# Gathering expert slots in columns by seven products instead of row by row, in a fused attention and soft-MoE kernel

## The chip, the cores and the metric

One core of a Trainium2 chip runs the kernel. The time is device microseconds of one execution; runs of the kernel before lay between 424.82 and 426.81 us. Work is shared by TensorE (PE in the profile; PEld are its weight loads), VectorE (DVE), ScalarE (ACT), GpSimd (POOL) and SyncE (SP), which issues the transfers. Each engine takes its instructions in order, and a semaphore wait holds up all that is queued behind it.

## The reference, cut to what matters

Two batches of 1024 tokens of 256 numbers go through a cross attention, a grouped feed forward, a sigmoid cross attention and last a soft mixture of experts, each added onto the input. The change lies in the last:

```python
xn = rms_norm(layernorm(x), gamma_x)            # (b, 1024, 256)
se = rms_norm(slot_embeds, gamma_slot)          # 8 x 128 = 1024 slots
logits = einsum('bsd,etd->bset', xn, se)
dispatch = softmax(logits, axis=1)              # over the tokens
slots = einsum('bsd,bset->betd', xn, dispatch)  # gather: (b, 1024 slots, 256)
h = gelu(slots @ w1)                            # 256 -> 1024
processed = h @ w2                              # 1024 -> 256
combine = softmax(logits over all slots)
out = einsum('bnd,bsn->bsd', processed, combine)
```

## The kernel before

All is in float32. A batch's 1024 tokens are eight tiles of 128; `xh` holds the normalised tokens (without gamma_x), `xhT` the same transposed, `seT` the transposed slots with the gammas folded in. The last layer runs per batch b through these stages:

- `logits(b, s)`: for token tile s, two PSUM banks of 512 slots (4 matmuls of 512 columns, L256); DVE stores the negated logits to `lg` with the row's minimum and keeps the running maximum over the tokens in `rmax`; ACT writes the exponentials for the combine weights to `ec` (L279), with their row sums in `zc`.
- `largest`/`spread` (batch 0, with TensorE) or `largest_by_moves`/`spread_by_moves` (batch 1, with transfers) turn `rmax` into `mb`, the maximum of each slot in all partitions. `less` adds `mb` to a tile of `lg` (L395; on POOL, three tiles of batch 1 on DVE), and `dispatch` takes the exponential in place on ACT (L398).
- `gather(b, c)`: slots 128 at a time, c = 0 to 7. Eight matmuls (L409, output `psl`) use a 128 x 128 piece of `lg` as weights and `xh` as moving operand. `xh` is 258 wide: two columns of ones give the sum of the exponentials beside each slot. DVE divides by that sum. Chunks 0 to 3 are transposed by DVE and two transfers, chunks 4 to 7 by TensorE (`turn_slots`, L450, output `pst`), with gamma_x multiplied in.
- `hidden(b)`: slots @ w1 and gelu, by Strassen-Winograd's seven products of halves (28 matmuls of 512 columns, L515, `pmh_a`, `pmh_b`, `pmh_c`); `sum_slots` and `sum_weights` make the sums of halves. A product that shares terms is added onto the bank of another, in PSUM.
- `processed(b)`: h @ w2, and `combined(b)`: the combine with `ec`, seven products each (112 matmuls of 128 columns each, L616, `pp` and `pc`). The sums of halves of their operands are made by DVE (L627), in place.
- `turn(q, h)` transposes a half of four tiles of `ec` for `combined`: four DVE transpositions (L308) and 16 transfers on SP (L325).

The order on TensorE is that of the code: logits of both batches, gather(0), hidden(0), processed(0), combined(0), then the same for batch 1. Inside `tc.manual_schedule` the engines that are named keep the order in which the code issues; elsewhere a scheduler orders them, ACT excepted in this last layer. While gather(0) runs, POOL and DVE take away the maxima of batch 1 and ACT takes its exponentials, so that all of batch 1's `lg` is ready long before gather(1). On ACT, `dispatch(1, 7)` stands ahead of hidden(0)'s first copy (L545).

Of the kernel before, what the change touches and what calls it, by code (L numbers as in the profile page):

```python
# [44 lines left out]
XW = D + 2  # L45
SQ = 32
R4 = P // SQ
IN_ORDER = {mybir.EngineType.DVE, mybir.EngineType.PE}
# [4 lines left out]
def tile_kernel(  # L53
# [50 lines left out]
    gx = const.tile([P, DC], FP, name="gx")  # L104

# [110 lines left out]
    def norm_tokens(q):  # L216
# [12 lines left out]
        xh = keep[q // QB].tile([P, QT, XW], FP, tag=f"xh_{q % QB}", name=f"xh_{q}")  # L229
        nc.gpsimd.memset(xh[:, :, D:XW], 1.0)  # L230
        for t in range(QT):
            nc.vector.tensor_scalar(
                xh[:, t, 0:D], xq[q][:, t, :], mv[:, t, 0:1], f[:, t : t + 1],
                ALU.subtract, ALU.mult,
            )
        xhs[q] = xh

    def turn_tokens(q):
        xhT = pools["mw"].tile([P, DC, QN], FP, tag="xhT", name=f"xhT_{q}", bufs=3)
        tr = pools["mw"].tile([P, R4, DC, QT, SQ], FP, tag="tr", name=f"tr_m_{q}", bufs=2)  # L240
        turned(xhs[q], xhT, tr)
        xhTs[q] = xhT

    def logits(b, s):
# [5 lines left out]
        lg = keep[b].tile([P, NSLOT], FP, tag=f"lg_{s}", name=f"lg_{b}_{s}")  # L250
        lgs[b][s] = lg
        nm = stat.tile([P, 2], FP, tag="nm", name=f"nm_{b}_{s}")
        for n in range(NSLOT // 512):
# [16 lines left out]
            if s == 1:  # L270
                nc.vector.scalar_tensor_tensor(
                    rm, lgs[b][0][:, ts(n, 512)], -1.0, pl, ALU.mult, ALU.max
                )
            elif s > 1:
                nc.vector.tensor_tensor(rm, rm, pl, ALU.max)  # L275
        if t == 0:

            ecs[q] = keep[b].tile([P, 2, QT, 512], FP, tag=f"ec_{q % QB}", name=f"ec_{q}")
# [9 lines left out]
    trs = {}  # L288

    def turn(q, h, late=False, move=True):  # L290
# [4 lines left out]
        if q < QB:  # L295
            tr = pools["m12"].tile(
                [P, R4, EC // 2, QT, SQ], FP, tag="tr", name=f"tr_{q}_{h}", bufs=2
            )
        else:

            if h == 0:
                trs[q] = keep[0].tile(
                    [P, 2, R4, EC // 2, QT, SQ], FP, tag=f"ec_{q % QB}", name=f"tr_{q}"
                )
            tr = trs[q][:, h]
        half = ecs[q][:, h]
        for t in range(QT):
            ins = nc.vector.transpose(  # L308
# [3 lines left out]
            if late:  # L312
                tc.keep_in_program_order(ins)
        turned_squares[q, h] = tr
        if move:
            turn_moves(q, h)

    turned_squares = {}

    def turn_moves(q, h):  # L320
        half, tr = ecs[q][:, h], turned_squares[q, h]
# [8 lines left out]
    def largest(b):  # L330
# [9 lines left out]
        dg = diagonals[:, 0, 0 : EC * SQ].rearrange("p (c n) -> p c n", c=EC)  # L340
# [8 lines left out]
    def spread(b):  # L349

        mb = pools["md"].tile([P, NSLOT], FP, tag="mb", name=f"mb_{b}")
        to = mb.rearrange("p (c i n) -> p i c n", c=EC, i=R4)
# [12 lines left out]
        mbs[b] = mb  # L365

    moved = {}

    def largest_by_moves(b):

        w = pools["slp"].tile([P, DC, NSLOT], FP, tag="slT", name=f"max_{b}")
        sq = w[:, 0, :]
        nc.vector.transpose(sq, rmaxs[b])
# [19 lines left out]
    def less(b, s):  # L393
        engine = nc.vector if b == 1 and s in (3, 4, 5) else nc.gpsimd
        engine.tensor_tensor(lgs[b][s], lgs[b][s], mbs[b], ALU.add)  # L395
# [4 lines left out]
    slTs, prs, pts, sls, hss, m12s = {}, {}, {}, {}, {}, []  # L400

    pzs, trs_sl, gx_row, m1_sums = {}, {}, [], []

    def gather_from(b, c, tiles):
        if c not in pzs:
            pzs[c] = bank(f"psl_{b}_{c}", 0)
        pz = pzs[c]
        for s in tiles:
            nc.tensor.matmul(  # L409
                pz[:, 0:XW],  # L410
                lhsT=lgs[b][s][:, ts(c, P)],
                rhs=xhs[b * QB + s // QT][:, s % QT, :],
                start=(s == 0),
                stop=(s == ST - 1),
            )

    def gather(b, c):

        if b == 0 and c == 0:

            for tiles in (range(4), range(4, ST)):
                for i in range(3):
                    gather_from(b, i, tiles)
        elif b > 0 or c > 2:
            gather_from(b, c, range(ST))
        pz = pzs.pop(c)
        rz = stat.tile([P, 1], FP, tag="rz", name=f"rz_{b}_{c}")
        nc.vector.reciprocal(rz, pz[:, D : D + 1])
        sl = pools["m12"].tile([P, D], FP, tag="sl", name=f"sl_{b}_{c}", bufs=2)
        if c >= QT:  # L430
            nc.vector.tensor_scalar(sl, pz[:, 0:D], rz, None, ALU.mult)
            sls[c] = sl
            return

        nc.vector.scalar_tensor_tensor(sl, pz[:, 0:D], rz, gx_row[0], ALU.mult, ALU.mult)
        if c == 0:
            trs_sl[b] = pools["md"].tile(
                [P, R4, DC, QT, SQ], FP, tag="rmax", name=f"tr_sl_{b}"
            )
        square(sl, trs_sl[b], c)  # L440
        if c == QT - 1:
            from_squares(trs_sl[b], slTs[b][0], f"sl_{b}")

    def turn_slots(b, c):

        if c % 2 == 0:
            pts[c // 2] = bank(f"pst_{b}_{c // 2}", 1)
        pt = pts[c // 2]
        for dc in range(DC):
            nc.tensor.transpose(  # L450
                pt[:, ds(dc * 2 * P + (c % 2) * P, P)], sls[c][:, ts(dc, P)], ident
            )
        if c == EC - 3:
            for dc in range(DC):
                slots_out(b, c // 2, dc)

    def slots_out(b, c2, dc):
        nc.vector.tensor_scalar(
            slTs[b][1][:, dc, ts(c2 - 2, 2 * P)], pts[c2][:, ts(dc, 2 * P)],
            gx[:, dc : dc + 1], None, ALU.mult,  # L460
        )

    lefts, rights = [], {}
# [13 lines left out]
    def sum_slots(b):  # L480

        x, y = slTs[b]
        b11, b21 = in_order(x, 0), in_order(x, 1)
        b12, b22 = y[:, 0, :], y[:, 1, :]

        def by_square(v):
            return v.rearrange("p (t i n) -> p t i n", t=QT, i=R4)


        t0, t1_ = (  # L490
            keep[b].tile([P, QT, XW], FP, tag=f"xh_{i}", name=f"sl_sums_{b}_{i}").rearrange(
                "p t d -> p (t d)"
            )
            for i in range(2)
        )
        t1, t2, t4 = t0[:, 0:512], t0[:, 512:1024], t1_[:, 0:512]
        slots_out(b, EC // 2 - 1, 0)
        nc.vector.tensor_tensor(by_square(t1), by_square(b12), b11, ALU.subtract)
        slots_out(b, EC // 2 - 1, 1)
        nc.vector.tensor_tensor(t2, b22, t1, ALU.subtract)  # L500
        nc.vector.tensor_tensor(b12, b22, b12, ALU.subtract)
        nc.vector.tensor_tensor(by_square(t4), b21, by_square(t2), ALU.subtract)
        rights[b] = [b11, b21, b22, t4, t1, t2, b12]

    def hidden(b):
# [1016 lines left out]
```

## Time and profile before

| | |
|---|---|
| median of 3 runs | 426.32 us (424.82 to 426.81) |
| profiled execution | 424.86 us, span 423.0 us |
| PE busy | 414.6 us, 98% |
| DVE, ACT, POOL busy | 297.8, 134.4, 73.7 us |
| gathering matmuls (L409) | 256 records, 56.8 us |
| hidden(0), first matmul to last end | 239.2 to 266.3 us |
| gather(1), first to last | 315.8 to 344.3 us |
| hidden(1) ends, combined(1) ends on PE | 369.8 us, 419.8 us |
| granted TensorE clock | full in every stretch |

Busy time is the time in which an engine works on at least one instruction. A float32 matmul leaves two records, and records overlap in the pipeline, so the price of one is read from the distance of starts and not from its mean duration. L-numbers are lines of the kernel before.

### The profile page before, as it was taken

To read this page: it belongs to the slowest core of one execution; us is meant where nothing else is said; L and a number is where in the kernel's file an instruction comes from. 1 tells how busy PE (TensorE), PEld (TensorE's weight loads), DVE (VectorE), ACT (ScalarE), POOL (GpSimd) and SP (SyncE) were. 2 spreads that over 40 slices of the span, in tenths; PEclk is the share of its full clock that TensorE was granted. 3 is DMA by queue.
4 is the path that set the end of the run, shared out by engine and by line. 5 is a ranking of instruction groups with operands and counts; after the bars stand their busy time and mean duration, and the time that the engine had idled before them with its cause. 6 is when DMAs were issued, how large, how long until landed. Compare 5 with 4: busy or idle time off the path is not lost.

```text
span 423.0 us, 6257 instructions
## 1 busy us (share of the span) xinstructions
PE 414.6 (98%) x2270; PEld 309.2 (73%) x2270; DVE 297.8 (70%) x680; ACT 134.4 (32%) x273; POOL 73.7 (17%) x86
## 2 busy tenths in 40 slices
PE   8999999999999999999999899999999999999996
PEld 6889988887544454444488544999998864499996
DVE  2676978645578669978769856677985585465956
ACT  1145568513544512343640755300000014610000
POOL 2112333211111220104948800000000000000000
PEclk9999999999999999999999999999999999999999
DMA  6999983413533332120063663540022576610003
GB/s 256 417 416 426 383 350 135 164 50 108 149 101 105 47 49 31 29 40 2 0 212 129 114 95 58 89 67 2 0 89 44 119 129 98 98 25 2 2 0 101
DMA packets 99424, 50.02 MB, mean 118 GB/s; under 512 B 87873, under 2 KB 94401, under 8 KB 97857
## 3 DMA queue, kind: packets, MB, share of 16 engines
q1 hardware_dynamic: 99394, 49.63, 41.7%
q8 instruction: 18, 0.29, 0.3%
q14 instruction: 12, 0.10, 0.1%
HBM read 32.74 MB, written 6.30 MB: 92 GB/s over the span
## 4 chain that ended last, share of the span: by engine, by line
PE 77%; POOL 8%; DVE 6%; issue 3%; SPq 2%; DMA 2%; ACT 1%; POOLq 1%; DVEq 0%; ACTq 0%
PE pmt L909 12%; PE pp L616 12%; PE pc L616 12%; PE psl L409 7%; POOL lg L395 6%; PE pl L256 5%; PE pmh_b L515 5%; PE pq L1263 3%; PE po L937 3%; PE pmh_c L515 3%; PE pmh_a L515 2%; SPq L158 2%; PE psc L1085 2%; PE pf L1277 2%; PE po L1131 2%
## 5 line engine op out<-in xcount | busy, mean ns | idle before, releaser
L909 PE MATMUL pmt<-wg 128*128 128x256 f32 x256 | 57.8, 380 | 1.0 <-DVE wg L900 0.9
L409 PE MATMUL psl<-xh,lg 128*128 128x258 f32 x256 | 56.8, 380 | 0.0
L256 PE MATMUL pl<-seT,xhT 128*128 128x512 f32 x128 | 56.1, 594 | 0.2 <-DVE rmax L275 0.2
L909 PEld LDWEIGHTS pmt<-wg 128*128 128x128 f32 x256 | 47.8, 189 | 8.8 <-DVE wg L900 1.9
L409 PEld LDWEIGHTS psl<-xh,lg 128*128 128x128 f32 x256 | 48.1, 190 | 7.4 <-issue 0.5
L256 PEld LDWEIGHTS pl<-seT,xhT 128*128 128x128 f32 x128 | 24.1, 190 | 29.2 <-issue 25.7
L395 POOL TENSOR_TENSOR lg<-lg,mb 128x1024 f32<-128x1024 f32 x13 | 33.2, 2584 | 26.8 <-ACT mb L203 25.3
L279 ACT ACTIVATE ec<-lg,nm 128x1024 f32<-128x1024 f32 x16 | 18.4, 1148 | 39.8 <-DVE nm L264 38.0
L616 PEld LDWEIGHTS pp<-ms,mh 128*128 128x128 f32 x256 | 29.4, 192 | 1.4 <-issue 1.4
L616 PE MATMUL pp<-ms,mh 128*128 128x128 f32 x256 | 29.8, 275 | 0.0
L898 ACT ACTIVATE wg<-wg,less 128x255 f32<-128x255 f32 x56 | 23.3, 496 | 0.1
L1340 ACT ACTIVATE sg<-psg 128x512 f32<-128x512 f32 x32 | 16.5, 603 | 18.2 <-PE psg L1331 18.2
L616 PE MATMUL pp<-m_sums,mh 128*128 128x128 f32 x192 | 22.1, 275 | 0.0
L616 PE MATMUL pc<-pr,ec 128*128 128x128 f32 x192 | 22.1, 275 | 0.0
L398 ACT ACTIVATE lg<-lg 128x1024 f32<-128x1024 f32 x16 | 16.1, 1045 | 18.2 <-POOL lg L395 18.2
L616 PEld LDWEIGHTS pp<-m_sums,mh 128*128 128x128 f32 x192 | 21.8, 192 | 0.0
L616 PEld LDWEIGHTS pc<-pr,ec 128*128 128x128 f32 x192 | 21.8, 192 | 0.0
L545 ACT COPY mh<-pmh_a 128x512 f32<-128x512 f32 x8 | 4.6, 582 | 50.7 <-PE pmh_a L515 50.7
L627 DVE TENSOR_TENSOR mh<-mh,mh 128x1024 f32<-128x1024 f32 x16 | 18.5, 1218 | 2.8 <-PE pp L616 2.8
L308 DVE STREAM_TRANSPOSE tr<-ec 128x512 f32<-128x512 f32 x32 | 19.8, 674 | 0.0
L616 PE MATMUL pc<-pr_sums,ec 128*128 128x128 f32 x160 | 18.5, 275 | 0.0
L515 PE MATMUL pmh_a<-slT,ms 128*128 128x512 f32 x32 | 16.3, 596 | 2.1 <-ACT mh L545 2.1
(197 smaller groups left out, 663.4 us busy)
## 6 DMA issues: line engine op xcount, KB each, us to landing
wg<-in_wff_dram SPq DMA_DIRECT2D x5, 2052.0 KB, 9.9
ec<-tr SPq DMA_DIRECT2D x128, 64.0 KB, 2.3
wg<-in_wff_dram SPq DMA_DIRECT2D x4, 1026.0 KB, 13.0
xT<-in_xT_dram SPq DMA_DIRECT2D x4, 512.0 KB, 14.0
x<-in_x_dram SPq DMA_DIRECT2D x4, 512.0 KB, 16.2
d_a<-tr_a SPq DMA_DIRECT2D x4, 512.0 KB, 2.6
hTa<-d_a SPq DMA_DIRECT2D x16, 128.0 KB, 3.0
xhT<-tr_m SPq DMA_DIRECT2D x64, 32.0 KB, 2.0
```

The lines of the kernel that those rows point to most:

```text
L256: nc.tensor.matmul(pl, lhsT=xhTs[q][:, dc, ts(t, P)], rhs=in_order(seT[:, n], dc), start=(dc == 0), stop=(dc == DC - 1),)
L279: nc.scalar.activation(ecs[q][:, :, t, :], lg.rearrange("p (h n) -> p h n", h=2), AF.Exp, bias=nm[:, 1:2], scale=-1.0, accum_out=zcs[b][:, ...
L308: ins = nc.vector.transpose(tr[:, :, :, t, :].rearrange("p r c n -> p c r n"), half[:, t, :].rearrange("p (c r n) -> p c r n", c=EC // 2, ...
L395: engine.tensor_tensor(lgs[b][s], lgs[b][s], mbs[b], ALU.add)
L398: nc.scalar.activation(lgs[b][s], lgs[b][s], AF.Exp, scale=-1.0)
L409: nc.tensor.matmul(pz[:, 0:XW], lhsT=lgs[b][s][:, ts(c, P)], rhs=xhs[b * QB + s // QT][:, s % QT, :], start=(s == 0), stop=(s == ST - 1),)
L515: nc.tensor.matmul(to, lhsT=lefts[i][:, ts(j, P)], rhs=in_order(slTs[b][0], i) if i < 2 else rights[b][i], start=first, stop=True, skip_gr ...
L616: nc.tensor.matmul(to, lhsT=left(k, m), rhs=right[:, k, :], start=(k == 0), stop=(k == QT - 1),)
L627: nc.vector.tensor_tensor(dst, x, y, op)
L898: nc.scalar.activation(w, w, AF.Identity, bias=less[:, oc : oc + 1])
L909: nc.tensor.matmul(pm[:, ts(hc, D)], lhsT=w1g[:, oc, ts(hc, P)], rhs=w2g[:, oc, :], start=(oc == 0 and hc == 0), stop=(oc == OC - 1 and hc ...
L1340: nc.scalar.activation(sg[:, j, :], psgs[j], AF.Tanh, scale=0.5 * DH1**-0.5)
```

## The change

The gather becomes one matrix product with the slots in columns, slots^T = xh^T x lg, by Strassen-Winograd's seven products of halves. The left operand is halved by tokens (tiles 0 to 3, 4 to 7) and by features (128 each), the right one by tokens and by slots (512 each). A product is four matmuls, one per tile: weights are 128 features of a tile of `xh` or of a sum, the moving operand 512 columns of `lg`. Three banks a, b, c collect the products; p2 goes onto p1's bank, p7 and p4 onto p6's, p3 onto p5's, and DVE adds between banks where terms are shared.

- `sum_tokens(b)`: four additions of 512 columns on POOL make the sums of halves of `xh` (in `slT`, one in place). The sums of halves of `lg` (t1 to t4, four additions of 512 columns each, in place in `lg`) are on DVE for batch 0 and on POOL for batch 1.
- The columns of ones go: since a token's features sum to 0 after the layernorm, column 0 of `xh` is overwritten with ones after the transposition, so row 0 of the result holds the sums of the exponentials. `sums_of_slots` turns this row into reciprocals (two transpositions, a reciprocal, one more, a transfer out to DRAM and one that spreads it to all partitions, 512 KB), and `sum_slots` multiplies the slots by them. `fold_gamma` puts gamma_x into w1 and subtracts the missing feature's row from the others (one ACT, two DVE instructions of 1024 columns; one row of w1 is loaded to all partitions).
- TensorE's transpositions of slots (L450), DVE's square transpositions with their two transfers, and the three DVE subtractions of maxima go; all eight `less(1, s)` are on POOL.
- Order: the maxima of batch 0 are formed one tile earlier; the last logits tile of batch 1 is split in two and lies inside gather(0); the maxima of batch 1 come in hidden(0), and its `less` after them. The exponentials of batch 1 are issued on ACT after hidden(0). gather(1) is no stage of its own any more: its products stand between the products of processed(0) and combined(0). The turns of `ec` move to hidden(0), processed(0), combined(0), hidden(1) and processed(1), through two buffers that they share with the moved tokens, the maxima and the reciprocals of batch 1. The order of products inside `hidden` is changed. POOL and SP now keep the order of the code too.

```diff
-    def gather_from(b, c, tiles):
-            nc.tensor.matmul(
-                pz[:, 0:XW],
-                lhsT=lgs[b][s][:, ts(c, P)],
-                rhs=xhs[b * QB + s // QT][:, s % QT, :],
...
+    def sum_tokens(b):
+        a11, a12, a21, a22 = blocks(b)
+        s1, s2, s4 = (of_tiles(b, i) for i in (1, 0, 3))
+        nc.gpsimd.tensor_tensor(s1, a21, a22, ALU.add)
+        nc.gpsimd.tensor_tensor(a21, a11, a21, ALU.subtract)
+        nc.gpsimd.tensor_tensor(s2, s1, a11, ALU.subtract)
+        nc.gpsimd.tensor_tensor(s4, a12, s2, ALU.subtract)
+    def gather(b, side):
+        add = nc.vector if b == 0 else nc.gpsimd
...
+        def onto(key, left, first, cols, new=True):
+            for k in range(QT):
+                nc.tensor.matmul(
+                    banks[key], lhsT=left[:, k, :], rhs=lg[first + k][:, cols],
...
+        def tiles(to, at, x, y):
+            for k in range(QT):
+                add.tensor_tensor(
+                    lg[to + k][:, at], lg[x[0] + k][:, x[1]], lg[y[0] + k][:, y[1]], ALU.subtract
+                )
+        b11, b12, b21, b22 = (0, lo), (0, hi), (QT, lo), (QT, hi)
+        def p1():
+            nc.scalar.copy(place(b, 2), onto("a", a11, 0, lo))
+        def t1():
+            tiles(*b11, b12, b11)
+        def t3():
+            tiles(*b12, b22, b12)
+        def p5():
+            nc.scalar.copy(place(b, 1), onto("c", s1, 0, lo))
+        def t2():
+            tiles(*b11, b22, b11)
+        def p6():
+            u = onto("b", s2, 0, lo)
+            nc.vector.tensor_tensor(u, u, place(b, 2), ALU.add)
+            nc.vector.tensor_tensor(banks["c"], u, place(b, 1), ALU.add)
+        def p2():
+            onto("a", a12, QT, lo, False)
+        def c11():
+            nc.scalar.copy(place(b, 0), banks["a"])
+        def t4():
+            tiles(*b21, b21, b11)
+        def p3():
+            nc.scalar.copy(place(b, 2), onto("c", s4, QT, hi, False))
+        def p7():
+            u = onto("b", s3, 0, hi, False)
+            nc.vector.tensor_tensor(place(b, 3), u, place(b, 1), ALU.add)
+        def p4():
+            nc.scalar.copy(place(b, 1), onto("b", a22, QT, lo, False))
...
+    p1(); t1(); p5(); t2(); t3(); p6(); p2(); c11(); t4()     # gather(0), a call a line
+    logits(1, ST - 1, (0,))
+    first_sum_of_slots(0)
+    fold_gamma(0)
+    p3()
+    sums_of_slots(0)
+    fold_gamma(1)
+    sum_weights()
+    p7()
+    logits(1, ST - 1, (1,))
+    p4()
+    sum_slots(0, 0)
+    squares_of_max(1)
+    sum_slots(0, 1)
...
+    hidden(0, in_hidden_0)      # within: largest_by_moves(1), spread_by_moves(1), less(1, 0..7), turn(0, 0), turn(0, 1)
+    for s in range(3):
+        dispatch(1, s)
+    sum_tokens(1)
...
+    def in_processed_0(i):      # called after processed(0)'s product i
+        if i == 1:
+            for s in range(3, ST):
+                dispatch(1, s)
+        if i == 4:
+            p1(); t1(); t3(); turn(1, 1)
+        if i == 7:
+            p2()
+        if i == 5:
+            p5(); t2(); t4(); turn(2, 0)
...
+    def in_combined_0(i):       # called after combined(0)'s product i
+        if i == 2:
+            p6(); c11()
+        if i == 4:
+            p3(); first_sum_of_slots(1); sums_of_slots(1)
+        if i == 7:
+            p7(); turn(3, 0)
+        if i == 6:
+            p4(); sum_slots(1, 0)
+        if i == 5:
+            sum_slots(1, 1)
```

The order of the products in processed is 2, 1, 4, 7, 5, 6, 3 and in combined 1, 2, 4, 7, 6, 5, 3, before and after.

## The prediction

> **What bounds the kernel now.** I read the page's busy times first, then TensorE's waits, then the chain of waits, and last the rows of single lines and stretches for prices.
>
> ```profile
> PE 414.6 (98%) x2270; PEld 309.2 (73%) x2270; DVE 297.8 (70%) x680; ACT 134.4 (32%) x273; POOL 73.7 (17%) x86
> ```
>
> TensorE works in 414.6 of 423.0 us, so the matmuls themselves are the bound. Its waits, inside the part that changes, are two:
>
> ```profile
> PE pmh_a L515 <- ACT mh L545: 2.1, 1, 2.1
> PE pmh_b L515 <- DVE sl_sums L500: 0.7, 1, 0.7
> ```
>
> The chain shows where the first comes from, and what one matmul of each kind costs TensorE (a matmul leaves two records, a transposition one):
>
> ```profile
> 200.40 13.94 POOL lg L395 x6
> ...
> 229.46 12.25 POOL lg L395 x4
> 241.73 1.06 ACT lg L398
> 242.79 0.48 ACT mh L545
> 243.31 1.12 PE pmh_a L515 x2
> 244.44 0.86 PE pmh_b L515 x2
> ...
> 315.98 20.93 PE psl L409 x96
> 336.92 0.22 PE pst L450 x2
> ```
>
> POOL's subtraction of the maxima (L395), ACT's exponential of the last token tile behind it and a copy queued behind that held TensorE for 2.1 us. The price list: a gathering matmul of 258 columns is 20.93 / 48 = 0.436 us, one of 512 columns 0.86, a transposition 0.11. The rows of L395 and L498 tell what happens when POOL and DVE add at once (min/median/max ns):
>
> ```profile
> L395 POOL TENSOR_TENSOR lg<-lg,mb x13: 2348/2357/3359, 195.7 to 239.3; 128x1024 f32<-128x1024 f32 x13
> L395 DVE TENSOR_TENSOR lg<-lg,mb x3: 2342/2784/2786, 228.2 to 234.4; 128x1024 f32<-128x1024 f32 x3
> L498 DVE TENSOR_TENSOR sl_sums<-slT x2: 692/992/1292, 241.0 to 346.2; 128x512 f32<-128x512 f32 x2
> L627 DVE TENSOR_TENSOR mh<-mh,mh 128x1024 f32<-128x1024 f32 x16 | 18.5, 1218 | 2.8 <-PE pp L616 2.8
> ```
>
> A DVE addition of 1024 columns with both inputs in SBUF takes 1.22 us by itself and 2.78 beside POOL's; one of 512 takes 0.69 and 1.29. POOL's goes from 2.35 to 3.36. DVE's transpositions (2.45 us for four beside POOL, 2.48 without) and its additions from PSUM (0.68 either way) do not suffer.
>
> Last, the room that DVE has where batch 0 ends (stretches; columns are length, then busy of PE, PEld, DVE, ACT, POOL):
>
> ```profile
> 239.10:266.20 27.10, 25.04 (x65) 11.24 (x64) 16.56 (x26) 16.55 (x27) 2.60 (x2) 1.00 0.54 81
> 266.20:291.00 24.80, 24.80 (x223) 24.80 (x222) 16.81 (x20) 1.77 (x3) 0.00 (x0) 1.00 0.40 60
> 291.00:315.90 24.90, 24.90 (x225) 24.90 (x225) 23.20 (x46) 0.59 (x1) 0.00 (x0) 1.00 0.08 24
> ```
>
> POOL is silent from 241.7 on. In combined(0), DVE is full (23.2 of 24.9). That is what the change moves into.
>
> **The change, part by part.** The sum is against the profiled execution's 424.86 us (1.9 of it outside the span); the median of the runs is 426.32, and differences are carried over to it.
>
> Removed from TensorE: per batch 64 matmuls at 0.436 = 27.9 us and 8 transpositions at 0.11 = 0.9. Added: 7 products x 4 tiles = 28 matmuls of 512 columns at 0.86 = 24.1. That saves 3.8 + 0.9 = 4.7 per batch, 9.4 in both. The two waits (2.8) go as well, if nothing takes their place: TensorE then ends 12.2 us earlier. The rest asks what takes their place.
>
> First gathering. It starts when the logits of tile 6 are done, 207.1 (the last logits, 3.45 us, now lie inside it as filler). The maxima of batch 0 are formed one tile earlier, so POOL's eight subtractions run some 3.4 us earlier, 192.3 to about 211. Its p1 needs tiles 0 to 3 and those are ready. DVE's sixteen subtractions of 512 columns (0.69 alone, 1.29 until POOL stops near 211) stay under the 0.86 per matmul from then on: t1 begins at 208.7 and its fourth tile is ready near 213.3, when TensorE is at 213.1. I take 0.3 us. If POOL overlapped all sixteen, they would cost 16 x 1.29 = 20.6 us against 24.1 + 3.45 of TensorE, still covered, but with about 2 us of waits. The sums' row then takes transpositions, a reciprocal and two transfers; the like of them (maxima to mb, 221.99 to 227.07) took 5.1 us. Started at 228.2 they land at 233.3, before hidden(0) can start at 207.1 + 24.1 + 3.45 + 0.3 = 235.0. fold_gamma and the weights' sums on POOL (4 x 1.29) end by 234.7, before hidden(0)'s p5 and p6 ask for them. The new load of one number per partition and the splitting of the m12 load sit on SP where nobody waits: the weights are wanted at 224. The four sums of tokens for batch 0 on POOL (4 x 1.29 = 5.2) fall into its idle time between 158 and 168; I take 0, and at most about 1 if DVE's normalisation beside them were hindered.
>
> hidden(0), 28 x 0.86 = 24.1 as before. In its last quarter DVE transposes weights (two turns of 2.48) between its additions, so the last product waits for the last addition: I take 0.7 (between 0 and 2.5, one turn). It ends at 259.8, against 266.3 before.
>
> Second gathering, the heart of it. POOL's chain: the transposed maxima are reduced on DVE at 244.9, moved (5.5 us in the trace, 214.7 to 220.2), reduced again and spread (5.1): mb of batch 1 lands at 256.0. Then POOL has 8 subtractions of the maxima, 4 sums of tokens and 16 subtractions of tiles, in this order, and DVE has at the same time the sums of the second layer's weights and of processed(0) and combined(0). An addition of POOL lies between 2.35 (alone) and 3.36; I take 2.92, the mean of the five in the trace (14.59 us), where DVE's two-input work was a like share (three additions of 1.22 in 12 us; here six of 1.22 and four of 0.69 in 22). The eight end at 256.0 + 23.4 = 279.4. ACT's last exponential (1.06) and, queued behind all eight on ACT, the copy of p1 (0.6 and 0.2 to get there) follow: the gathering's p2 may start at 281.3. TensorE gets to it at 259.8 + 7.15 + 3.57 + 3.44 + 3.57 = 277.5 (16 matmuls of 128 columns are 3.57). **Wait 3.8.** By 2.35 it would be none, by 3.36 7.3.
>
> The sums of tokens and t1, eight of 512 columns at 1.29 x 2.92 / 2.35 = 1.6, end at 292.2; the last matmul of its p5 ends 0.9 later, 293.1. TensorE would be through it at 281.3 + 3.44 + 3.57 + 3.44 = 291.7. **Wait 1.4.** t3, t2 and t4 end by 312 and are asked for later than that, but for t2, which has about 3 us to spare.
>
> In combined(0) the gathering's p3 adds onto a bank that DVE must first fill, and this instruction stands behind DVE's four sums of 1024 columns and an accumulation of 1.65. With POOL beside part of them I take **1.0** (0 if POOL is through; 6 if all are slowed to 2.78). SP's queue has the turns (16 transfers each; 32 took 22.57 us, so 11.3 a turn) ahead of the second sums' row, and is through them at about 318, before the row is asked for at 321. hidden(1) loses its 0.7 wait. In processed(1) one more turn and one pair of sums stand on DVE, which is busy 15.5 of 25.0 there; no cost, or 1 at most if the turn's transfers are late.
>
> Sum: -9.4 - 2.8 + 0.3 + 0.7 + 3.8 + 1.4 + 1.0 = **-5.0 us**: 419.9 for an execution like the profiled one, **421.3** for the median.
>
> The Trainium skill (SBUF — State Buffer, "SBUF: two separate sides") says that DVE with two SBUF inputs and GpSimd hold a shared pair of ports one at a time, each for a whole instruction. By it a POOL addition with a DVE one always queued would cost 2.35 + 1.22 = 3.57 us, an estimate; the trace has 3.36 at most, which bears the rule out, and 2.92 on average. By 3.57 throughout, the wait at p2 would be 9.0 and not 3.8, and most of the gain gone. It is the rule that speaks against this change: it puts 28 additions on POOL just where DVE's two-input work is densest.
>
> **The rivals.**
> *All of it is hidden.* POOL's additions stay near 2.35, since DVE's additions come in bursts with turns and additions from PSUM between them; subtractions then end at 274.8 and the copy at 276.7, before 277.5. For it: DVE is busy only 16.8 of 24.8 in processed(0) in the trace. Against: combined(0) is full. It gives 426.3 - 12.2 = 414.1, with a wait or two about 416. Chance 0.28.
> *POOL and DVE block each other all the way, in the second gathering.* Each POOL addition 3.36 (1.84 for 512 columns), each DVE sum 2.78: p2 at 284.7 (wait 7.2), p5 3.0 more, p3 6.0, and 1.0 as above: 17.2 of waits, 12.2 saved, so 5.0 slower, 431.3. It decides once the waits together pass 12.2, which is POOL's additions at about 3.1 us with most of DVE's sums at double. For it: the upper ends of the L395 rows, 3359 and 2786 ns; against: DVE's share of two-input work is about a third. Chance 0.11.
> *The gain is eaten up exactly*, waits between 10 and 14 us, by the same mechanism or by mb landing 4 us later than 256.0 (each us there is one at p2): within 0.5%. Chance 0.13.
> The forecast itself has 0.48.
>
> **How the numbers follow.** The runs before span 424.82 to 426.81, so about 0.5% (2.1 us) is what can be told from no change. Faster by more: the forecast and the first rival, 0.76; within: 0.13; slower: 0.11. The range leaves out some of the lowest and the slow rival's far end: 414.3 to 427.5.
>
> **What would show it.** Right: 28 matmuls a batch at 0.86, TensorE's busy time near 405, a wait at the second gathering's p2 released by ACT's copy, behind exponentials that wait for POOL, and one at p5 released by POOL; POOL additions of batch 1 near 2.9. The first rival: additions at 2.35 and no such waits. The second: additions above 3.1, DVE sums near 2.8 and a long wait at p3. Wrong altogether: waits in the first gathering, or at hidden(0)'s start behind the sums' row, or a matmul into a filled bank costing more than 0.86.

## The result, and the profile after

The changed kernel takes 427.07 us (median of 20 runs, 425.21 to 428.78). The kernel before took 425.34 in the 20 runs beside them (424.82 to 426.83). The ratio is 1.003, with a 95% interval of 1.0015 to 1.0044: slower by 0.3%, within what I had called no change. The profiled execution is 425.61 us with a span of 423.8, against 424.86 and 423.0. I had forecast 421.3, which is 5.0 less than the 426.32 that the forecast started from.

The first line of the page after, busy times of the engines:

```profile
PE 408.9 (96%) x2110; PEld 281.8 (66%) x2110; DVE 324.6 (77%) x670; ACT 143.5 (34%) x285; POOL 119.0 (28%) x113
```

TensorE works 5.7 us less, and its chain ends 0.8 us later (420.64 instead of 419.84). So it waits more. TensorE's waits of the kernel after (us in total, times, longest):

```profile
PE pf L1360 <- DVE oT L1453: 2.9, 1, 2.9
PE psl_c L444 <- POOL lg L456: 2.4, 2, 2.2
PE pp L686 <- DVE mh L697: 2.1, 1, 2.1
PE psl_c L444 <- DVE psl_c L480: 1.6, 1, 1.6
```

The first is in a place that I had costed at nothing: the sigmoid attention's last output, 50 us ahead of the first gathering. Timelines show it (start, duration, what). POOL's token sums of batch 0 come right behind POOL's last small operation of a norm of the tokens:

```profile
152.66 1.27 POOL L426 TENSOR_TENSOR slT<-xh,xh 128x512 f32<-128x512 f32 x1
```

and beside them DVE's steps of that norm, on four numbers a partition:

```profile
152.73 1.22 DVE L229 TENSOR_TENSOR f<-f,rstd_m 128x4 f32<-128x4 f32 x1 [0.81 <-POOL rstd_m L130]
...
154.41 0.90 DVE L232 TENSOR_TENSOR f<-f,rstd_m 128x4 f32<-128x4 f32 x1
155.33 1.19 DVE L233 TENSOR_SCALAR f<-f 128x4 f32<-128x4 f32 x1
```

Before, these steps took 0.16 us each. The first of them:

```profile
152.73 0.16 DVE L224 TENSOR_TENSOR f<-f,rstd_m 128x4 f32<-128x4 f32 x1 [0.81 <-POOL rstd_m L125]
```

The attention output that TensorE waits for (L1453) stands behind them in DVE's queue; it starts at 157.11 and not at 154.29.

The other waits are in the second gathering. POOL there:

```profile
275.32 6.62 POOL L401 TENSOR_TENSOR lg<-lg,mb 128x1024 f32<-128x1024 f32 x2
281.90 2.24 POOL L426 TENSOR_TENSOR slT<-xh,xh 128x512 f32<-128x512 f32 x1
...
290.73 6.91 POOL L456 TENSOR_TENSOR lg<-lg 128x512 f32<-128x512 f32 x4
297.60 16.59 POOL L456 TENSOR_TENSOR lg<-lg,lg 128x512 f32<-128x512 f32 x12
```

The last two subtractions of maxima, beside DVE's sums of 1024 columns, take 3.3 us each; the mean of all eight is 2.80, and one takes 2.36 where DVE does not hinder it. An addition of 512 columns takes 2.2 us in the token sums (1.27 at 152.66); the mean is 1.73 in t1 and 1.38 in the rest. The four matmuls of p5 are paced by t1's four tiles: TensorE is free at 290.66 and done with p5 at 298.66, 8.0 us for 3.44 us of work, so 4.56 lost. DVE's sums of 1024 columns, 1.22 us on average before, are (busy, mean ns of one):

```profile
L697 DVE TENSOR_TENSOR mh<-mh,mh 128x1024 f32<-128x1024 f32 x16 | 29.6, 1913 | 0.6 <-PE pp L686 0.6
```

The whole stretch from 256 to 320 (length, then busy of PE, PEld, DVE, ACT, POOL, and the granted clock):

```profile
256.00:320.00 64.00, 59.17 (x369) 45.15 (x367) 59.54 (x53) 17.70 (x24) 54.52 (x28) 0.97 0.56 90
```

and in the kernel before:

```profile
256.00:320.00 64.00, 64.00 (x492) 57.97 (x491) 47.10 (x79) 8.80 (x16) 0.00 (x0) 1.00 0.28 50
```

DVE was busy for 47.1 us of it and POOL for none. Now both are nearly full. Last, a column that had been 1.00 all through the kernel before, the granted clock, around the wait at p5 (length, PE busy, clock):

```profile
292.00:294.00 2.00, 0.98 (x1) 0.77 0.00 0
294.00:296.00 2.00, 1.85 (x3) 0.50 0.00 0
296.00:298.00 2.00, 2.00 (x5) 0.88 0.11 17
```

This stretch at half clock lasted 3.4 us (from the three rows) but cost p5 hardly anything: t1's last tile is ready at 297.64 (290.73 + 6.91), and one matmul of 0.86 later p5 is through at 298.66, or 0.16 more than that.

The ledger on TensorE: saved 12.2 as reckoned; new waits of 2.9 (attention output), 1.0 (first gathering: 0.6 at p5 and 0.4 before hidden(0)), 0.3 (inside hidden(0): 24.4 us from 238.55 to 262.92, for 24.1 us of matmuls), 2.1 (p7 of processed(0)), 0.4 (p2), 4.6 (p5) and 1.6 (p3). Together 12.9, and so 0.7 later; 0.8 was measured.

### The profile page after: what moved, and what is told of

Its sections match the earlier page's. It is cut to its first block, busy times and chain, and to the rows that moved or that the text cites. A ratio compares the mean times of both kernels' runs of the same rounds, so it can differ in the third digit from the quotient of the medians.

```text
span 423.8 us, 5977 instructions
## 1 busy us (share of the span) xinstructions
PE 408.9 (96%) x2110; PEld 281.8 (66%) x2110; DVE 324.6 (77%) x670; ACT 143.5 (34%) x285; POOL 119.0 (28%) x113
## 4 chain that ended last, share of the span: by engine, by line
PE 74%; POOL 10%; DVE 7%; issue 6%; DMA 1%; ACT 0%; SPq 0%; DVEq 0%; POOLq 0%; ACTq 0%
PE pmt L991 12%; PE pl L274 12%; PE pc L686 9%; PE pp L686 7%; POOL lg L401 5%; PE pq L1346 3%; PE psl_c L444 3%; PE po L1019 3%; PE pf L1360 3%; PE psl_b L444 3%; PE pmh_b L585 2%; PE psg L1414 2%; PE psc L1168 2%; PE poT L1446 2%; PE po L1214 2%
## 5 line engine op out<-in xcount | busy, mean ns | idle before, releaser
L401 POOL TENSOR_TENSOR lg<-lg,mb 128x1024 f32<-128x1024 f32 x16 | 41.1, 2607 | 36.7 <-DMA mb<-mrow 21.6
L697 DVE TENSOR_TENSOR mh<-mh,mh 128x1024 f32<-128x1024 f32 x16 | 29.6, 1913 | 0.6 <-PE pp L686 0.6
L274 PE MATMUL pl<-seT,xhT_late 128*128 128x512 f32 x64 | 28.4, 594 | 0.0
L274 PE MATMUL pl<-seT,xhT 128*128 128x512 f32 x64 | 28.1, 594 | 0.0
L274 PEld LDWEIGHTS pl<-seT,xhT_late 128*128 128x128 f32 x64 | 12.0, 190 | 14.7 <-issue 14.0
L274 PEld LDWEIGHTS pl<-seT,xhT 128*128 128x128 f32 x64 | 12.1, 190 | 14.3 <-issue 11.5
L444 PE MATMUL psl_c<-lg,slT 128*128 128x512 f32 x32 | 16.6, 658 | 4.5 <-POOL lg L456 2.4
L686 PEld LDWEIGHTS pc<-pr_sums,ec 128*128 128x128 f32 x160 | 18.5, 192 | 1.4 <-issue 1.2
```

The lines of the kernel that those rows point to most:

```text
L274: nc.tensor.matmul(pl, lhsT=xhTs[q][:, dc, ts(t, P)], rhs=in_order(seT[:, n], dc), start=(dc == 0), stop=(dc == DC - 1),)
L401: nc.gpsimd.tensor_tensor(lgs[b][s], lgs[b][s], mbs[b], ALU.add)
L444: nc.tensor.matmul(banks[key], lhsT=left[:, k, :], rhs=lg[first + k][:, cols], start=new and k == 0, stop=k == QT - 1, skip_group_check=no ...
L686: nc.tensor.matmul(to, lhsT=left(k, m), rhs=right[:, k, :], start=(k == 0), stop=(k == QT - 1),)
L697: nc.vector.tensor_tensor(dst, x, y, op)
```

## The experiments

Theories: (1) POOL's early token sums hold up DVE's small steps; (2) in the second gathering POOL's and DVE's additions hold each other up, and p5 and p3 wait for the ends of the two queues; (3) waits also cost clock behind them. Against (1): the order on DVE alone. Against (2): POOL slow by itself, or the products too dear. Medians and spans, "before" being the runs of the kernel before on the same chip:

| kernel | median (range) | span, profiled | clock, runs | before |
|---|---|---|---|---|
| the change | 427.07 (425.21 to 428.78) | 423.8 | 0.984 to 0.996 | 425.34 |
| late token sums | 422.93 (422.71 to 423.28) | 421.2 | 0.992 to 1.000 | 426.24 |
| and split token sums | 424.18 (422.25 to 425.72) | 420.5 | 0.987 to 0.995 | 426.24 |
| and p3's bank first | 417.43 (416.18 to 420.25) | 414.4 | 0.991 to 1.000 | 425.78 |
| no DVE sums (work left out) | 419.65, one run | 417.8 | 0.996 | 426.24 |
| no POOL additions (left out) | 419.02, one run | 417.2 | 1.000 | 426.24 |
| late sums, later turn | 422.66 (422.14 to 423.02) | 420.9 | 0.992 to 1.000 | 425.78 |
| all orders together | 417.48 (416.98 to 418.11) | 415.1 | 0.996 to 1.000 | 425.78 |

### Late token sums

```diff
-            sum_tokens(0)
+            sum_tokens(0, xhs[NQ - 1][:, :, 0])
...
+        if after is not None:
+            nc.gpsimd.tensor_tensor(place(b, 1)[:, 0:QT], after, after, ALU.add)
```

> Edit: a 4-element addition that reads the last tokens' finished tile is put ahead of batch 0's four token sums on POOL, so that they run about 27 us later (near 180 instead of 152.7), where DVE has no small additions between SBUF operands that TensorE waits for. Theory (POOL's sums hold DVE's 4-element steps of the token norm up): those steps fall back to about 0.16 us (1.22, 0.90 and 1.19 us in the changed kernel), TensorE's wait of 2.9 us for the attention output's scaled tile goes, and the time falls by 2.9 us, from 427.1 to about 424.2; the span from 423.8 to about 420.9. Rival (the order of the work on DVE, not POOL, makes that tile late): DVE's order is unchanged here, so the steps may shorten but the wait stays above 2 us and the time stays within 0.7 us of 427.1. Rival (the sums then hinder something else at 180 to 186, such as the transposed maxima): a new wait of 1 us or more near 190 to 210 takes the gain back.

DVE's timeline, the same steps (line numbers behind an edit shift by a few in the experiments; these don't):

```profile
152.74 0.16 DVE L229 TENSOR_TENSOR f<-f,rstd_m 128x4 f32<-128x4 f32 x1 [0.81 <-POOL rstd_m L130]
...
153.55 0.17 DVE L233 TENSOR_SCALAR f<-f 128x4 f32<-128x4 f32 x1
```

The order on DVE is the same, the steps fall to 0.16 us, and the wait for the attention output is gone. The sums run at 177 to 182 at 1.28 us and hinder nothing there: DVE's work beside them reads PSUM. The span falls by 2.6, the median by 4.1. Theory (1) holds. The rest of the median fits lost clock: behind this wait TensorE could run at half clock as well ("Waits filled with matmuls" shows such an execution).

### Split token sums

```diff
     sum_tokens(1)            # of batch 1, now only the sum that p5 needs
...
-            p1(); t1(); t3(); turn(1, 1)
+            p1(); t1(); sum_more_tokens(1); turn(1, 1)
...
-            p5(); t2(); t4(); turn(2, 0)
+            p5(); t2(); t3(); t4(); turn(2, 0)
```

> Edit: the one before, and POOL's order in the second gathering changed: of batch 1's token sums only the one that p5 needs stands ahead of t1, the other three stand behind it, and t2 stands ahead of t3. No work is added or left out. Theory (p5 waits for POOL's chain of 8 subtractions, 4 sums and 4 subtractions, each 512-column one 1.7 to 2.2 us beside DVE's sums): t1 ends three sums, about 6.5 us, earlier, TensorE's stretch of p5 (4.6 us longer than the products need) shrinks to the products' 3.4 us with at most 0.5 us of waiting, and the time falls by a further 4 us against the edit before, to about 420. Rival (what is gained at p5 is lost again behind it: p6 waits for t2, or p3 for the bank that DVE fills): the wait before p3, 1.6 us, grows to 3 us or more, or p6 waits for over 2 us, and the time stays within 1 us of the edit before.

p5's waits are gone (TensorE passes from 290.69 to 294.29 through it), but the span falls by 0.7 only, and the median is 1.25 higher. This is the rival in kind: the wait before p3 grows from 1.1 to 2.85, where it had 3 or more, and p7 of processed(0) also waits 1.4 longer than without the split (3.7 against 2.3). TensorE's and DVE's timelines:

```profile
318.43 3.70 PE L452 MATMUL psl_c<-lg,slT 128*128 128x512 f32 x8 [2.85 <-DVE psl_c L488]
```

```profile
308.64 4.49 DVE L705 TENSOR_TENSOR ec<-ec,ec 128x1024 f32<-128x1024 f32 x2
313.05 2.35 DVE L705 TENSOR_TENSOR ec<-ec 128x1024 f32<-128x1024 f32 x2
315.32 1.65 DVE L864 SCALAR_TENSOR_TENSOR x<-pc,zc,x 128x256 f32<-128x256 f32 x4
...
317.68 0.70 DVE L488 TENSOR_TENSOR psl_c<-psl_b,slT 128x512 f32<-128x512 f32 x1
```

The addition that fills p3's bank stands at the end of DVE's queue. It came at 318.39 with the wait at p5, and comes at 317.68 without it. So p5's wait was covering one behind it. The longer wait at p7 is another thing: DVE's first sum of processed(0) took 2.55 us here and 0.84 without the split, which is taken up under "Waits filled with matmuls".

### p3's bank first

```diff
         if b == 0:
             first_sums(b)
+            after(2)          # gather(1)'s p6 and the two additions into banks
             sum_last(b)
...
         add(0, both, p1)
-        after(2)
```

> Edit, on top of the split token sums: in combined(0) DVE does the two additions that fill the bank of p3 right behind the first pair of its own 1024-column sums, ahead of the second pair and of four accumulations. Theory (what the split won at p5 was lost at p3, since DVE's queue beside POOL's additions has no slack there and the bank stands at its end): the additions start near 313.1 instead of 316.9, TensorE's wait of 2.9 us before p3 becomes 0 to 0.3, the span goes from 420.5 to about 417.7 and the median from 424.2 to about 421.4. Rival (it only moves on: the sums now put back make the product after p3 wait): a wait of 2 us or more at the products behind p3, and no change in the time.

```profile
312.32 3.70 PE L452 MATMUL psl_c<-lg,slT 128*128 128x512 f32 x8
```

No wait before p3, and none behind it. The median falls by 6.8, more than expected: 3 of it are the wait, and the profiled execution also passed p7's wait at 2.2 (3.7 in two pieces in the kernel before this one) and kept the clock. Against the kernel before the ratio is 0.981 (0.978 to 0.984), against the change itself 417.43 to 427.07. No work is saved by these three edits; they are order alone (and one 4-element addition more).

### One side's additions left out

```diff
# no DVE sums: processed(0)
-        sums(a11, a11, a21, SUB)        # and the other three
# no POOL additions: batch 1
-        nc.gpsimd.tensor_tensor(s1, a21, a22, ALU.add)   # and the other three sums, t1 to t4
```

> Edit, against the changed kernel itself: the four sums of batch 0's hidden activations (eight additions of 1024 columns on DVE) in processed(0) are left out, so the products there take the unsummed halves. Theory (POOL's additions in the second gathering take long because each takes turns with a DVE addition): the last subtractions of maxima, the four token sums and t1 fall towards what they take where DVE is not adding, 2.35 us and 1.27 us; p5's extra 4.6 us and p7's 2.1 us go. Span about 6 us shorter, some 417. Rival (POOL is as slow there by itself, or held up by ACT or transfers): token sums stay above 2.0 us and t1's above 1.6 us, and p5 waits as before.

> Edit, against the changed kernel itself: batch 1's four token sums and sixteen subtractions of tiles on POOL are left out (p5, p6 and p3 take unsummed operands); the eight subtractions of maxima stay. Theory (DVE's sums of 1024 columns are held up by whatever POOL adds beside them): the ones that run after POOL's last subtraction of maxima fall from 1.7 to 2.75 us to 1.2 us; p5 does not wait; p7's wait, which lies beside the subtractions of maxima, stays at 1 to 2.1 us; p3's 1.6 us becomes 0 to 0.5. Span 5 to 6 us shorter than 423.8. Rival (p7's wait comes from the token sums behind the subtractions): p7's wait goes too.

POOL's timeline without DVE's sums:

```profile
281.45 1.26 POOL L426 TENSOR_TENSOR slT<-xh,xh 128x512 f32<-128x512 f32 x1
...
286.60 4.93 POOL L456 TENSOR_TENSOR lg<-lg 128x512 f32<-128x512 f32 x4
```

2.2 us become 1.26, and t1's 1.73 become 1.23; p5 and p7 do not wait. DVE's sums without POOL's additions, in the stretch where both had run:

```profile
286.79 2.35 DVE L701 TENSOR_TENSOR mh<-mh,mh 128x1024 f32<-128x1024 f32 x2
```

That is 1.2 each (1.95 each in the change), p5 and p3 do not wait, and p7 still waits 2.2, since the maxima's subtractions beside it stay. Both spans came within a microsecond of what was expected (417.8 and 417.2). Theory (2) holds on both sides, in one run of each: neither engine is slow by itself.

### A later turn, and all orders together

```diff
             sum_rights(right, t1, t2, t4)
-            turn(1, 0)
...
         sums(a11, a11, a21, SUB)
+        if b == 0:
+            turn(1, 0)
```

> Edit, on top of the late token sums alone: in processed(0) DVE's four transpositions of the second quad's weights (2.5 us) go behind the first pair of sums, the pair that TensorE's p7 waits for. Theory: p7's wait of 2.3 us goes and the half clock behind it too (28 matmuls in 5.0 us, 3.4 at full clock), but p5's end is set by POOL's chain, which is as before: TensorE then waits for ACT's copy before p2 (about 2 us) and longer for POOL at p5, so p5 ends within 0.5 us of 296.6, and the time stays within 0.7 us of 422.9. Rival (each wait on TensorE costs for itself): the span falls by 3.5 us, to 417.7.

> Edit: late token sums of batch 0, split token sums of batch 1, the bank of p3 filled first and the transpositions behind the first pair of sums, all together. No work is added or left out. Theory (the waits follow from the order on DVE and POOL, and with POOL's chain out of the way p7's wait counts): p7's 2.6 and 1.1 us go, p2 waits up to 1 us for ACT, p5 up to 1.5 us for POOL, and p3 up to 1 us for DVE; span 415 to 416.5, median 417 to 418.5, some 8 us less than the kernel before. Rival (DVE and POOL together have no more room between 257 and 320): p3's wait comes back with 2 us or more, and the time is that of e5_bank_first.

With late token sums alone, p7's wait of 2.3 went and p2 waited longer for ACT, which stands behind POOL's subtractions:

```profile
PE psl_a L446 <- ACT slT L465: 2.7, 1, 2.7
```

p5 ended at 297.06 (296.62 without the edit), and the time is the same, as the theory had it. But not quite for its reason: t1's last tile came at 294.60, and p5's matmuls ran at a granted clock of 0.50 from 290 to 296 and so ended later than POOL asked for. Runs at a clock of 1.000 took no less (422.67 and 422.78); what holds these is not known. With all orders together p7's wait is gone too and the same 2.7 us stand at p2, where 1 at most was expected: 417.48, no better than 417.43. The last wait has only changed its place. What sets it is the chain of the maxima's landing (257), eight subtractions of 2.8, an exponential and a copy.

### One subtraction on DVE

```diff
-            for s in range(ST):
+            for s in range(ST - 1):
                 less(1, s)
...
+            less(1, ST - 1, nc.vector)
+            dispatch(1, ST - 1)
             turn(1, 0)
```

> Edit, on top of e8_all: the last of batch 1's eight subtractions of maxima goes from POOL to DVE, behind the pair of sums that p7 waits for; its exponential follows it. Theory (with p7's wait gone, p2 waits 2.7 us for POOL's eight subtractions, each 2.8 us by turns with DVE's, ACT's exponential and ACT's copy behind it): POOL is through with seven at about 276.8, the copy ends near 279.7, p2's wait is 1 to 1.5 us, no half clock follows it, and the median is 1 to 2 us less than 417.5. Rival (DVE's sums behind it are now late): TensorE waits 1 us or more for DVE at p5 of processed(0), and the time is the same or more.

417.49 (417.35 to 417.59), clock 0.999 and 1.000. The time did not fall. p2's wait went from 2.7 to 0.4, but p7 waited 1.6 for DVE again, and two other places 0.2 and 0.3. p7's wait is not the rival's doing: the moved subtraction stands behind the pair of sums that p7 waits for, and starts (276.68) only as the pair ends. The pair itself was late (276.76 against 275.07 with all orders), because DVE's first sum of processed(0) took 2.82 us here and 0.82 in the kernel with all orders:

```profile
259.03 2.82 DVE L705 TENSOR_TENSOR m_sums<-ms 128x512 f32<-128x512 f32 x1
```

So this run doesn't tell what the moved subtraction is worth; the next section takes up the first sum.

### Waits filled with matmuls

```diff
+            for _ in range(32 if (b, i) == (0, 7) else 0):     # 10 in the second, on the kernel with p3's bank first
+                nc.tensor.matmul(to[:, 0:P], lhsT=ones, rhs=ones, start=True, stop=True)
```

> Edit, on top of e5_bank_first: 32 matmuls of 128 columns on constants (about 3.6 us, their result overwritten) stand ahead of p7's product, in the time in which TensorE waits for DVE there. Work is only added. Theory (a wait of some 2.3 us or more in TensorE is followed by about 3.3 us at half the clock, which costs p7 1.6 us, in some executions and not in others): no half clock behind p7's wait, its 28 matmuls take 3.4 us instead of 5.0, the time falls by about 1.6 us against the kernel without the filling and spreads less from run to run (mean granted clock 0.995 and more throughout). Rival (the clock does not follow the waits, or its loss is covered by DVE): the same time as without the filling, or up to 1.5 us more.

> Edit, on top of e5_bank_first: ten matmuls of 128 columns on constants ahead of p7's product, in place of the 32 of e7_filled. A matmul of this shape took 0.223 us there, so ten are 2.2 us and fill the wait of 2.2 us without lengthening it. Theory (a wait of over 2 us in TensorE is followed in some executions by half the clock): no execution shows a mean clock below 0.998, the time stays within 0.5 us of the best of e5_bank_first, 416.2, in all runs, and its median is about 1.1 us less than 417.4. Rival (the clock falls for another reason): medians alike, some runs at 0.995 and 417.5 as before.

What they are after is seen in p7 of processed(0), in the change and with late token sums (TensorE's timelines):

```profile
279.78 3.39 PE L686 MATMUL pp<-ms,mh 128*128 128x128 f32 x28 [2.10 <-DVE mh L697]
```

```profile
277.06 5.02 PE L688 MATMUL pp<-ms,mh 128*128 128x128 f32 x28 [2.28 <-DVE mh L699]
```

The same matmuls behind nearly the same wait took 1.63 us longer, at a granted clock of 0.56 to 0.59 in the stretches from 278 to 282. The wait for the attention output has such a pair too. Behind it 12 records of L1360 take 2.86 us in the profile of the change, at full clock, but in that of the kernel without DVE's sums, whose code is the same up to there, they take 4.39 us behind the same wait of 2.89. That is 1.53 us more, at a granted clock of 0.50 from 160 to 162.

With 32 matmuls I had mis-sized the filling: they took 7.15 us (0.223 each, not 0.11), so the kernel is slower, 420.55. But all five runs have a clock of 0.999 or 1.000. With ten (2.23 us) the clock stays at 0.999 or more in four runs, but the time was 416.51 once and 417.5 to 417.6 three times, so the expectation on the time failed. The profiled run is one of the latter; DVE's timelines of it and of the kernel without filling show another alternative, which has nothing to do with the clock:

```profile
259.06 2.58 DVE L705 TENSOR_TENSOR m_sums<-ms 128x512 f32<-128x512 f32 x1
```

```profile
258.64 0.77 DVE L705 TENSOR_TENSOR m_sums<-ms 128x512 f32<-128x512 f32 x1
```

DVE's first sum of processed(0) either starts ahead of POOL's second subtraction of maxima or behind it, and 1.8 us of p7's wait hang on that. All twelve profiles of the change and its variants agree. In eight the sum starts with the subtraction or up to 0.24 us ahead of it, and takes 0.67 to 0.84 us; in four (split token sums, ten matmuls, one subtraction on DVE, a stage of its own) it starts 0.05 to 0.36 us behind it and takes 2.55 to 2.86. That this is what parts the runs at 416.5 from those at 417.5 is not shown, since one execution of each kernel is profiled.

The same filling in the kernel before, in its wait of 2.1 us at the start of hidden(0), settles the clock:

```diff
         def p2(j):
+            if b == 0 and j == 0:      # nine matmuls into the bank that p6 overwrites next
+                for _ in range(9):
+                    nc.tensor.matmul(banks["b", 0][:, 0:P], lhsT=ones, rhs=ones, start=True, stop=True)
             onto("a", 1, j, first=False)
```

> Edit, against the kernel before: nine matmuls of 128 columns on constants (2.0 us) into a bank that is overwritten right after, in TensorE's wait of 2.1 us at the start of hidden(0). Work is only added. Theory (the kernel before has two times, near 425.0 at a mean clock of 1.000 and near 426.5 at 0.996, because this wait is followed by half the clock in some executions): all runs lie within 0.4 us of 425.0 at a clock of 0.998 and more. Rival (the two times have another cause): runs near 426.5 at 0.996 appear as before, in about half of all.

```profile
241.31 2.17 PE L552 MATMUL pmh_b<-ones 128*128 128x128 f32 x18
243.47 1.13 PE L515 MATMUL pmh_a<-slT,ms 128*128 128x512 f32 x2
```

Twelve runs lie between 424.58 and 425.12, none near 426.5. Beside them the kernel before had twelve runs between 424.70 and 425.32 at a clock of 0.999 or 1.000, and five between 426.35 and 426.80 at 0.996. More work on TensorE took the upper times away. With five in seventeen at the upper time, twelve runs without one would come by chance about once in 65 trials, an estimate. So a wait of 2.1 us is followed by lost clock in some executions and not in others, at about 1.6 us a time; one stretch of 3.4 us at half clock would make just such a mean of 0.996 over 425 us. Theory (3) holds, though in the kernel before no slow execution was profiled.

### The second gathering in a stage of its own

```diff
-        if i == 4:
-            p1(); t1(); t3(); turn(1, 1)      # and the rest between the products
...
 combined(0, in_combined_0)
+    p1(); t1(); p5(); t2(); t3(); p6(); p2(); c11(); t4()     # as gather(0), t1 to t4 on DVE
+    first_sum_of_slots(1); p3(); sums_of_slots(1); p7(); p4(); sum_slots(1, 0); sum_slots(1, 1)
 hidden(1, in_hidden_1)
```

> Edit, on top of the late token sums of batch 0: the second gathering is taken out from between batch 0's last products and stands by itself between combined(0) and hidden(1), in the order of the first gathering, its sixteen subtractions of tiles on DVE as there; POOL keeps the maxima's subtractions and the token sums. Theory (the waits of the second gathering come from POOL's chain and DVE's queue beside batch 0's last products, and its products by themselves save what was reckoned): no wait at p5 for POOL and none at p3 for combined(0)'s sums, 2.3 and 1.1 us and the half clock at p5; p7 of processed(0) still waits about 2.2 us for DVE, since POOL's maxima stay beside it; new are 0.6 us at p5 for t1, as in the first gathering, and 1 to 3 us before hidden(1), whose operands now have only p7 and p4 ahead of them to cover the sums' transfers. Span 416 to 419.5, median 418 to 421.5; so between the late token sums alone (422.9) and e5_bank_first (417.4). Rival (what costs is the gathering's seven products themselves, or their additions wherever they stand): the time stays at 422.9 or above. Other rival (its own stage is the better place even against the mended order): 416 or less.

430.86 (430.53 to 431.45): none of the theories expected that. TensorE's waits:

```profile
PE pp L688 <- DVE mh L699: 6.6, 2, 4.5
PE pc L688 <- DMA ec<-tr: 4.1, 1, 4.1
```

The gathering itself waits 0.5 and 0.9 us for DVE and has no wait for POOL, as expected. But without p1, p2, p5 and p6 between them batch 0's own products come earlier than DVE's sums beside POOL's maxima, and than the turned weights' transfers. The gathering's products had been the cover for these. Clock went as well: it is 0.50 all the way from 274 to 284, behind a wait of 4.5 us, and falls again from 308 to 311, behind one of 4.1; the runs' clocks are 0.984 to 0.988. DVE's first sum is a late one here too (2.86). So with this order of DVE's sums and of the turns, the place between the products is the better one; a stage of its own with its own mended order was not tried.

## Why the prediction was wrong, point by point

**The failed step, in short.** The mechanism at the second gathering was foreseen, and the saving. Two terms were wrong: the token sums of batch 0 were put at 0 and cost 2.9, and the wait at p5 was put at 1.4 and was 4.56. These two are 6.1 us of the 5.7 by which the sum missed; the others nearly cancel.

**The saving, right.** 9.4 us of matmuls were reckoned; with the waits mended TensorE is busy for 406.1 us (p3's bank first) instead of 414.6, which is 8.5. The two old waits went.

**Token sums of batch 0 on POOL: the step that failed first.** "Fall into its idle time between 158 and 168; I take 0, and at most about 1 if DVE's normalisation beside them were hindered." POOL was idle, but already from 152.7 on, and the scheduler put the sums right behind POOL's last small operation of the norm, beside DVE's chain of 4-element steps, and that chain stood ahead of the copy out of PSUM that TensorE needed: 2.9 us, shown by moving the sums alone. I had looked only at the engine that the work goes to. The bound of 1 us was too low as well: three steps of about 0.16 us became 1.22, 0.90 and 1.19.

**Second gathering's p2: the mechanism, not quite the place.** POOL's subtractions took 2.80 on average (2.92 reckoned), and mb came 3.5 us later than 256.0, of which 2.9 are the earlier wait. Of the 3.8 us at p2, 2.1 stood at p7 of processed(0), where DVE's sums were late (the first pair took 3.3 us each beside POOL's subtractions), and 0.4 at p2; 1.3 less in all. The later-turn runs show that the two are one: take p7's away, and p2 has 2.7.

**p5: the term that was mis-sized most.** 1.4 was reckoned, 4.56 measured. The eight additions of the token sums and t1 were put at 1.6 each, 12.8 us; they took 15.7 (281.90 to 297.64), and these 2.9 us are nearly all of the miss. I had scaled 512-column additions by the mean found for 1024 columns, 1.29 x 2.92 / 2.35 = 1.6. But an addition on POOL that takes turns with a 1024-column sum of DVE loses much the same for either length: 2.35 became 3.3, and 1.27 became 2.2. The mean of 2.80 or 2.92 also has subtractions beside DVE's transpositions and 512-column sums in it. The Trainium skill (SBUF — State Buffer, "SBUF: two separate sides") has the pair of ports held by one engine for a whole instruction. By that rule, one addition of POOL's with one of DVE's would be 1.27 + 1.22 = 2.49 for 512 columns and 2.35 + 1.22 = 3.57 for 1024, as estimates. The runs have 2.2 and 3.3: near to taking turns for both, and about 0.3 below it for both.

**p3 and the first gathering.** 1.6 against 1.0, and 1.3 for the first gathering and hidden(0) against 1.0. The price of p3 was near, but I read it as a term by itself. In the split run it grew to 2.9 as p5's went: DVE's queue was the limit there. So the two waits were not independent terms: what is mended at p5 comes back in part at p3. My reading of DVE's four transpositions as unhindered beside POOL rested on two rows in which POOL worked for about half of the time; it held, 2.48 us in the change with POOL busy throughout (270.73).

**The sum.** -12.2 with 12.9 of waits, against 7.2 reckoned; 419.9 becomes 425.6, and the profiled execution has 425.61. This is the rival "the gain is eaten up exactly", waits between 10 and 14, to which I had given 0.13; but 2.9 of it came from a place that no rival named. "POOL and DVE block each other all the way" came in places only: 3.3 where DVE's 1024-column sums stood beside the subtractions, 2.80 on average. The carry-over from the profiled execution to the median, 1.4 us, held by luck: both kernels' medians contain lost clock. Before, it was the 2.1 us wait; after, there are three waits of over 2 us. The drop behind p5's wait is in the profile above, and drops behind the other two were profiled in variants (the attention output's without DVE's sums, p7's with late token sums). That the lower clocks of most runs of the change itself (0.991 and less, 426.6 and more) come from these fits their times, except for one run of 427.18 at 0.996, but none of them was profiled.

## What to carry to other kernels

When work moves to an idle engine, ask what its operations hold up on the neighbour that adds from the same memory, and whether a short chain on that neighbour stands ahead of what TensorE waits for; put such work where the neighbour reads PSUM or transposes. Where two queues run full side by side, the waits aren't independent: mend one and the next appears, so find the last of them in the queue that is full, and move what TensorE needs to the head of it. Three changes of order turned 427.07 us into 417.43 (1.003 of the kernel before into 0.981) without an instruction less.

## What the hardware showed that I had not expected

Waits of TensorE of 2.2 to 2.9 us were followed, in some executions and not in others, by 3.4 us at half the granted clock, which costs up to 1.6 us a time; the two times of the kernel before say the same of its wait of 2.1 us. Filling the wait with matmuls that nobody needs removed it in all of 12 and of 5 runs. The Trainium skill (TensorE: Matmul & The Clock Gate, "Part 1: The HAM clock gate") states that the clock goes to half after an idle window of about 3.4 us; here it fell to half behind shorter waits as well (2.2 at p5 of the change, 2.3 and 2.6 at p7 with late and with split token sums, 2.9 at the attention output without DVE's sums, and once behind two waits of 1.2 and 1.1 with one matmul between them, p5 with late token sums). DVE's operations on four numbers a partition, one of them with a single input from memory and a constant (L233), took up to 1.22 us beside POOL's additions, over seven times their 0.16.
